# A two-layer graph kernel on one core: four pieces of a step's side work get other places in the order, one 8-bit tile a third buffer, and one addition another engine

## The chip, the core and the metric

The kernel runs on one core of one Trainium2 chip. A core has a matrix engine (TensorE; PE in the profile, its weight loads PEld), VectorE (DVE), ScalarE (ACT), GpSimd (POOL) and SyncE (SP), which issues most of the loads. Each engine takes its instructions strictly in its own order; between engines there are only semaphores. The metric is device time in microseconds (us): the median of the runs of one kernel. Lower is better.

## The reference, cut to what matters

There are N = 3327 rows x of width D = 512 and an adjacency matrix adj (0 or 1, about 1% ones). Twice a graph attention layer is applied, then a residual and a layer norm; a second, binary layer and another layer norm follow:

```python
def _gat_layer(x, W, adj):
    Wh, Ws = jnp.split(x @ W, 2, axis=-1)
    a = jax.nn.softmax(Wh @ Ws.T, axis=-1) * adj
    return jax.nn.leaky_relu(a @ Wh + x, 0.01)
h = _gat_layer(_gat_layer(x, W[0], adj), W[1], adj)
x = _layernorm(x + h)                      # "x +" is the input added to finished rows
bw, ba = sign(weight), maximum(sign(x), 0)
out = _layernorm(x + relu(adj @ (ba @ bw.T)))
```

The work is in `Wh @ Ws.T` (3327 x 3327 scores), the exponential of them, the mask, and `a @ Wh`.

## The kernel before, in words

**Tiling.** Rows are cut into 26 tiles of 128, and pairs of tiles make NQ = 13 groups g of 256 columns. A *step* is a pair (g, q): a 256 x 256 block of scores. The list `steps` has 169 of them, all q of g = 0 first. Each layer of attention (`attention(l, att)`, l = 0 and 1) runs over v, the index of the step whose values are multiplied (`values`, L1103 and on: seven products of a Strassen scheme, each 128x256, in `one`, L1120). Scores are made 31 half steps ahead (`LOOK`), so v starts below zero; those early steps have no values to multiply and are about half as long.

**Scores.** Of the 26 half steps of a chunk of two groups, 20 are made by `quad_scores` (five blocks of 4 half steps, 26 products each, L820), the other six by an ordinary Strassen scheme (L781). The products accumulate in banks of PSUM called P, Q, R, S, T, V (quad) or X, Y, Z; the pool `ps_ch` has only three. An intermediate result is taken from a bank, and more products then go into it, or another name gets the bank. It is taken out either by a ScalarE copy (`keep_as`, L826) or by a VectorE addition (`out`, L832; these are *a block's additions*). TensorE cannot add into the bank again until that is done. So a late L832 or L826 stops TensorE.

**The side work of a step**, for a block that was scored before:
- `shift`, L1044, VectorE: subtracts the column maximum (`beside`, which lies in PSUM) from the block, for step v+3.
- `exponential`, L1050, ScalarE, step v+3 (for q = 0 also L1049, the first term of the running total).
- `running`, L1055, VectorE: adds the block to the running total, step v+2.
- `masked`, L1060, VectorE: times adj, step v+2; behind it `sums`, L1093 to L1096, four GpSimd operations that make Strassen's left sides in a tile with three buffers.
- `narrow`, L1068, ScalarE: casts the adjacency block to 8 bits into the tile `adj_b` (two buffers); `degrees`, L1073, GpSimd; `exact`, L1083, VectorE; one step later `keep_blocks`, L1076, a GpSimd DMA that writes the 8-bit block to HBM. This happens in about every second step.
- `maximum`, L879, VectorE; `column_max` (L972 to L996), once for each group.
- When a group's last q is done, `take_out` (L1146 to L1157) reads its values from PSUM, and `finish` hands out one item a step: `scaled` (L1185), `leaky` (L1193), `stored` (in layer 1 the addition of the input, L1202, and then a GpSimd DMA, L151), `statistics` (L1215, L1216), `signs` (L1222, L1229).

**The order** is written by hand. Each step collects pairs of a place and a function, sorts them by place, and calls them; every engine's queue then is that order. Place 0 is the step's first product, 1 its last. Products have places too: value i has (i + 0.5)/7, the n-th product of a quad block (n + 0.5)/6.5 counted over its four half steps, and its addition comes 0.082 later. The lines that place the side work (L1379 to L1385):

```python
at = 0.12 if v >= 0 else 0.33 if v < -2 else 0.45
work += [(0.0, lambda: shift(*s3)), (at, lambda: exponential(*s3))]
...
work += [(0.2, lambda: running(*s2)), (0.48, lambda: masked(*s2))]
...
(0.6, lambda: narrow(*of)), (0.61, lambda: degrees(*of)), (0.66, lambda: exact(*of)),
...
if later and (last or v + 2 not in blocks or len(later) > 5 - v % NQ // 2):
    work += [(0.8, later.pop(0))]
```

`later` holds what `finish` handed out, `after` what goes to the next step (`keep_blocks` at 0.5). After both layers the binary layer's products (`aggregate`, L1471, and `linear`, L1564) end the kernel.

Of the kernel before, what the change touches and what calls it, by code (L numbers as in the profile page):

```python
# [11 lines left out]
F8 = mybir.dt.float8e4  # L12
# [3 lines left out]
ALU = mybir.AluOpType  # L16
# [3 lines left out]
P = 128  # L20
# [3 lines left out]
HW = CW // 2  # L24
# [21 lines left out]
def kernel(  # L46
# [8 lines left out]
    nc = tc.nc  # L55
# [6 lines left out]
    NQ = NT // 2  # L62
# [8 lines left out]
    def halves_of(c):  # L71
        return [g for g in (2 * c, 2 * c + 1) if g < NQ]

    def dense(c):
        return 0 < c and len(halves_of(c)) == 2 and c < NC

    def half_tiles(g):

        return (2 * g, 2 * g + 1)
# [16 lines left out]
    def slot(shape, dtype, name):  # L96
        return ring.tile(shape, dtype, tag="s", bufs=SBUFS, name=name)
# [609 lines left out]
    def attention(l, att):  # L707
# [173 lines left out]
        def scores(c, q, s):  # L881

            if dense(c) and q // 2 in quads:
                if (q % 2, s) == (0, 0):
                    quad_scores(c, q // 2)
                return []
            mine = halves_of(c)
            if s == 0:
                for i in mine:
                    sc[i, q] = slot([P, 2, HW], F32, f"s_{l}_{i}_{q}")  # L890
            w = len(mine) * P
            lo, hi = sc[mine[0], q][:, :, :w], sc[mine[-1], q][:, :, HW - w :]
            c11, c21, c12, c22 = lo[:, 0], lo[:, 1], hi[:, 0], hi[:, 1]

            def copied(name, bank):
                ch[name] = att.tile([P, w], F32, tag=name, bufs=1, name=f"{name}_{l}_{c}_{q}")
                nc.scalar.copy(ch[name], ch[bank])

            def z1():
                product(c, q, "Z", A11, B11, True)  # L900
                ch["X"] = ps_ch.tile([P, w], F32, tag="ch", name=f"pX_{l}_{c}_{q}")
                nc.scalar.copy(ch["X"], ch["Z"])

            def y5():
                product(c, q, "Y", S1, T1, True)
                copied("p5", "Y")

            def z6():
                product(c, q, "Z", S2, T2, False)
                copied("u2", "Z")  # L910

            def y3():
                product(c, q, "Y", S4, B22, False)

            def add12():
                nc.vector.tensor_tensor(c12, ch["Y"], ch["u2"], ALU.add)

            def z7():
                product(c, q, "Z", S3, T3, False)

            def add22():
                nc.vector.tensor_tensor(c22, ch["Z"], ch["p5"], ALU.add)  # L922

            def x2():
                product(c, q, "X", A12, B21, False)
                nc.scalar.copy(c11, ch["X"])

            def z4():
                product(c, q, "Z", A22, T4, False)
                nc.scalar.copy(c21, ch["Z"])  # L930

            if s == 1:

                after.append((-0.05, lambda: maximum(mine[0], q)))
                if q == NQ - 1:

                    plans = [
                        ((1, -0.04), (1, 0.2), (1, 0.6), (2, 0.16), (2, 0.17)) if mine[0] == 0
                        else ((1, -0.04), (1, 0.2), (1, 0.7), (2, 0.02), (2, 0.3)),
                        ((2, 0.68), (5, 0.83), (6, 0.83), (7, 0.83), (8, 0.83)),  # L940
                    ]
                    for i, plan in zip(mine, plans):
                        for (n, at), do in zip(plan, column_max(i)):
                            early.setdefault(v + n, []).append((at, do))
            if s == 0:
                return [(0.06, z1), (0.31, y5), (0.56, z6), (0.81, y3), (0.94, add12)]
            return [
                (0.02, z7), (0.15, add22), (0.35, x2), (0.68, z4),
            ] + [(0.62, lambda i=i: maximum(i, q)) for i in mine[1:]]
# [91 lines left out]
        def shift(g, q):  # L1041
            s = sc[g, q]
            at = beside[l][:, 0:1]
            nc.vector.tensor_tensor(s, s, at.to_broadcast([P, 2, HW]), ALU.subtract)  # L1044

        def exponential(g, q):
            if q == 0:
                total[g] = att.tile([P, 2, HW], F32, tag="total", name=f"total_{l}_{g}")
                nc.scalar.activation(total[g], sc[g, q], AF.Exp)  # L1049
            nc.scalar.activation(sc[g, q], sc[g, q], AF.Exp)  # L1050

        def running(g, q):

            if q > 0:
                nc.vector.tensor_tensor(total[g], total[g], sc[g, q], ALU.add)  # L1055

        def masked(g, q):

            s = sc[g, q]
            nc.vector.tensor_tensor(s, s, adj[g, q], ALU.mult)  # L1060
            sums(g, q, s)

        def narrow(g, q):

            t = adj[g, q, "b"] = att.tile(
                [P, 2, HW], F8, tag="adj_b", bufs=2, name=f"ab_{l}_{g}_{q}"
            )
            nc.scalar.copy(t, adj[g, q], saturate=False)  # L1068

# [89 lines left out]
        def finish(g):  # L1159
# [6 lines left out]
            mine = half_tiles(g)  # L1166
            held = {}
# [29 lines left out]
            def stored(i):  # L1197
                t, hh = mine[i], hs[i]
                r = rows(t)
                span = slice(t * P, t * P + r)  # L1200
                if last:
                    nc.vector.tensor_tensor(hh[:r], hh[:r], held[i, "x0"][:r], ALU.add)  # L1202
                load_rows(nc.gpsimd, h_d[span, :] if last else x1_d[span, :], hh, r)

            def residual(i):
# [56 lines left out]
        if last:  # L1262
# [14 lines left out]
            for n, e in enumerate(some):  # L1277
                at = n * (n1 - n0) / len(some)
# [59 lines left out]
        mine = [i for i, e in enumerate(steps) if e[1] % L == l]  # L1338
# [9 lines left out]
        for v in range(-LOOK - 4, len(steps)):  # L1348
            u = v + LOOK

            if 0 <= v + WS - 1 < len(steps):
                load_ws(*steps[v + WS - 1])
            if 0 <= v + 4 < len(steps):
                load_adj(*steps[v + 4])
            if v + 4 in blocks and (v + 4 < 0 or blocks[v + 4] != steps[v + 4]):
                load_adj(*blocks[v + 4])
            if 0 <= u + 2 < len(ahead):
                c, q, h = ahead[u + 2]
                if h == 0:
                    load_xs(c, q)  # L1360
            if u == -4:
                load_gs(0, 0, 7)

            c, i = divmod(u, 2 * NQ)
            if 0 <= c < NC - 1 and 22 <= i < 25:
                load_gs(c + 1, 2 * i - 44, 1 if i == 24 else 2)
            if dense(c) and i == 0 and quads:
                for n, at, do in query_sums(c):
                    early.setdefault(v + n, []).append((at, do))
            work, after = after, []  # L1370
            if 0 <= c < NC - 1 and i == 2 * NQ - 1:
                work += [
                    (at, lambda c=c, n=n: load_gs(c + 1, n)) for n, at in ((5, 0.43), (6, 0.8))
                ]
            if 0 <= v + 3 < len(steps):
                s3 = steps[v + 3]
                if not any(s3):
                    work.append((-0.02, lambda: spread(0)))
                at = 0.12 if v >= 0 else 0.33 if v < -2 else 0.45  # L1379
                work += [(0.0, lambda: shift(*s3)), (at, lambda: exponential(*s3))]  # L1380
                if s3[1] == NQ - 1 and s3[0] + 1 < NQ:
                    work.append((0.9, lambda: spread(s3[0] + 1)))
            if 0 <= v + 2 < len(steps):
                s2 = steps[v + 2]
                work += [(0.2, lambda: running(*s2)), (0.48, lambda: masked(*s2))]  # L1385
            if v + 2 in blocks:
                of = blocks[v + 2]
                work += [
                    (0.6, lambda: narrow(*of)), (0.61, lambda: degrees(*of)),
                    (0.66, lambda: exact(*of)),  # L1390
                ]
                after.append((0.5, lambda of=of: keep_blocks(*of)))
            if later and (last or v + 2 not in blocks or len(later) > 5 - v % NQ // 2):
                work += [(0.8, later.pop(0))]
            if 0 <= u < len(ahead):
                work += scores(*ahead[u])
            if v >= 0:
                work += values(*steps[v])
            work += early.get(v, [])
            for _, do in sorted(work, key=lambda e: e[0]):  # L1400
                do()
            if v >= 0 and steps[v][1] == NQ - 1:
                later += finish(steps[v][0])
            if last:
                load_products(v)
# [337 lines left out]
```

## Time and profile before

| | |
|---|---|
| median of 3 runs | 2499.78 us (2499.44 to 2500.13) |
| the profiled execution's own time | 2498.87 us |
| its span, first to last instruction | 2497.1 us |
| granted TensorE clock | 0.999 |
| TensorE busy | 2471.4 us (99%), 12052 matmuls |
| VectorE / ScalarE / GpSimd busy | 2031.8 (81%) / 852.9 (34%) / 1505.6 us (60%) |
| DMA | 635.89 MB |

A row of a group reads: line, engine, operation, written<-read tiles, shapes, count, then busy us and mean ns of one, then the idle time of the engine just before these instructions and what ended it. A row of the timeline reads: start, length, engine, line, operation, tiles, count, and in brackets the idle time before and what ended it. The trace shows each 128x256 matmul as 379 ns long, though the next one starts 216 ns after it: they overlap, so lost time of TensorE is read from the starts.

### The profile page before, as it was taken

The numbers are of one execution on the slowest core, as the hardware profiler recorded it, in microseconds if no ns is written. First come the engines' busy times: TensorE is split into PE (matmuls) and PEld (weight loads), VectorE is DVE, ScalarE is ACT, GpSimd is POOL, SyncE is SP. The second block draws the span as 40 slices with busy tenths as digits, with TensorE's granted clock in tenths as the row PEclk, the third lists the DMA queues.
The fourth block names the chain that finished last, engine by engine and source line by source line (L and its number), as shares of the span: only waits on it lengthen the run. The fifth ranks groups of instructions, "written<-read, shape, count | busy, mean of one in ns | idle before, by whom it ended". The sixth has DMA issues, their size and how long they took to land.

```text
span 2497.1 us, 39159 instructions
## 1 busy us (share of the span) xinstructions
PE 2471.4 (99%) x12052; PEld 2140.4 (86%) x12052; DVE 2031.8 (81%) x4005; ACT 852.9 (34%) x2127; POOL 1505.6 (60%) x2487
## 2 busy tenths in 40 slices
PE   9999999999999999999999999999999999999998
PEld 7888888888888888998888888888888888899886
DVE  6864788888988988768886588988889898888876
ACT  3333433333333333322233333333333333332234
POOL 3772566767677676545677256666666666655631
PEclk9999999999999999999999999999999999999999
DMA  6976767676677766897797676767767677688985
GB/s 209 322 267 222 249 236 253 233 262 236 239 253 236 266 230 231 294 317 258 244 334 270 225 260 220 269 223 265 241 232 270 227 268 240 230 283 301 317 279 174
DMA packets 318149, 635.89 MB, mean 255 GB/s; under 512 B 34317, under 2 KB 182405, under 8 KB 317934
## 3 DMA queue, kind: packets, MB, share of 16 engines
q1 hardware_dynamic: 289454, 540.93, 64.9%
q0 software_dynamic: 28480, 92.40, 9.6%
q8 instruction: 98, 1.61, 0.3%
q14 instruction: 117, 0.96, 0.1%
HBM read 521.98 MB, written 111.21 MB: 254 GB/s over the span
## 4 chain that ended last, share of the span: by engine, by line
PE 93%; DVE 4%; DMA 1%; issue 1%; ACT 1%; POOL 0%; SPq 0%; ACTq 0%; DVEq 0%; POOLq 0%
PE acc L1120 38%; PE pZ L781 9%; PE pP L820 6%; PE pQ L820 6%; PE pY L781 5%; PE pR L820 4%; PE pZ_wh L547 4%; PE pZ_g L612 3%; PE agg L1471 3%; PE pX L781 2%; PE pY_wh L547 2%; PE pY_g L612 2%; PE pT L820 2%; PE pS L820 1%; PE pm L439 1%; PE pV L820 1%
## 5 line engine op out<-in xcount | busy, mean ns | idle before, releaser
L1093 POOL TENSOR_TENSOR as<-s 128x128 f32<-128x128 f32 x338 | 210.9, 624 | 563.3 <-DVE s L1060 424.6
L1120 PE MATMUL acc<-ws,s 128*128 128x256 f32 x1352 | 402.3, 379 | 0.0
L1120 PE MATMUL acc<-ws,as 128*128 128x256 f32 x1352 | 380.5, 379 | 0.0
L1120 PE MATMUL acc<-wh,s 128*128 128x256 f32 x1352 | 380.0, 379 | 0.0
L1050 ACT ACTIVATE s<-s 128x512 f32<-128x512 f32 x338 | 213.2, 631 | 399.5 <-DVE s L1044 397.6
L1073 POOL TENSOR_TENSOR deg<-deg,adj 128x256 fp8e4<-128x256 fp8e4 x338 | 263.6, 780 | 44.5 <-DMA adj<-in_adjT_dram 29.7
L1120 PEld LDWEIGHTS acc<-ws,as 128*128 128x128 f32 x1352 | 251.4, 190 | 37.0 <-issue 3.1
L1120 PEld LDWEIGHTS acc<-wh,s 128*128 128x128 f32 x1352 | 252.5, 190 | 32.5
L1120 PEld LDWEIGHTS acc<-ws,s 128*128 128x128 f32 x1352 | 251.4, 190 | 33.1
L1055 DVE TENSOR_TENSOR total<-total,s 128x512 f32<-128x512 f32 x312 | 263.4, 844 | 0.0
L1060 DVE TENSOR_TENSOR s<-s,adj 128x512 f32<-128x512 f32 x338 | 242.5, 717 | 2.6 <-DMA adj<-in_adjT_dram 0.3
L879 DVE TENSOR_TENSOR top<-top,s 128x512 f32<-128x512 f32 x286 | 224.0, 786 | 23.4 <-ACT s L930 21.3
L781 PE MATMUL pZ<-ga,xs 128*128 128x256 f32 (+1 forms) x1096 | 234.3, 340 | 2.1 <-DVE s L922 1.7
L1044 DVE TENSOR_TENSOR s<-s,beside 128x512 f32<-128x512 f32 x338 | 227.7, 674 | 2.5 <-ACT beside L1039 2.5
L1094 POOL TENSOR_TENSOR s<-s 128x128 f32<-128x128 f32 x338 | 207.4, 614 | 26.7
L781 PEld LDWEIGHTS pZ<-ga,xs 128*128 128x128 f32 x1096 | 191.4, 190 | 26.4 <-DVE s L922 2.5
L1095 POOL TENSOR_TENSOR as<-s 128x128 f32<-128x128 f32 x338 | 191.3, 566 | 26.5
L1096 POOL TENSOR_TENSOR as<-s,as 128x128 f32<-128x128 f32 x338 | 185.3, 548 | 26.5
L1120 PE MATMUL acc<-wh,as 128*128 128x256 f32 x676 | 201.2, 379 | 0.0
L826 ACT COPY s<-pP 128x256 f32<-128x256 f32 x200 | 74.3, 372 | 249.6 <-PE pP L820 217.3
L1120 PEld LDWEIGHTS acc<-wh,as 128*128 128x128 f32 x676 | 125.7, 190 | 20.2 <-issue 3.6
L1076 POOL DMA_DIRECT2D adj_d<-ab x169 | 94.0, 556 | 78.5 <-ACT ab L1068 58.0
(274 smaller groups left out, 4969.6 us busy)
## 6 DMA issues: line engine op xcount, KB each, us to landing
ws<-ws_d SPq DMA_DIRECT2D x338, 512.0 KB
adj<-in_adjT_dram SPq DMA_DIRECT2D x351, 256.0 KB
xs<-xq_d SPq DMA_DIRECT2D x100, 832.0 KB
xs<-xs_d SPq DMA_DIRECT2D x82, 512.0 KB
xs<-xs_d SPq DMA_DIRECT2D x82, 384.0 KB
gs_d<-gsp POOLq DMA_DIRECT2D x84, 256.0 KB, 3.8
xq_d<-xq POOLq DMA_DIRECT2D x20, 832.0 KB, 4.7
ga<-gs_d SPq DMA_DIRECT2D x54, 256.0 KB
```

The costliest lines, as they stand in the source:

```text
L781: nc.tensor.matmul(ch[bank], xs[c, q, a][:, k], query(c, b)[:, k], start=(start and k == 0), stop=(k == 1), skip_group_check=True,)
L820: nc.tensor.matmul(bank[b], xs[c, i, f"x{r}"], right, start=r in begins, stop=True, skip_group_check=True,)
L879: nc.vector.tensor_tensor(top[i], top[i], t, ALU.max)
L1044: nc.vector.tensor_tensor(s, s, at.to_broadcast([P, 2, HW]), ALU.subtract)
L1050: nc.scalar.activation(sc[g, q], sc[g, q], AF.Exp)
L1055: nc.vector.tensor_tensor(total[g], total[g], sc[g, q], ALU.add)
L1060: nc.vector.tensor_tensor(s, s, adj[g, q], ALU.mult)
L1073: nc.gpsimd.tensor_tensor(deg[:, g], deg[:, g], adj[g, q][:, a], ALU.add, saturate=False)
L1093: nc.gpsimd.tensor_tensor(s3, a11, a21, ALU.subtract)
L1094: nc.gpsimd.tensor_tensor(a21, a21, a22, ALU.add)
L1095: nc.gpsimd.tensor_tensor(s2, a21, a11, ALU.subtract)
L1120: nc.tensor.matmul(acc[g][i // 2][:, i % 2], a[i], b[i], start=(q == 0 and i % 2 == 0), stop=(q == NQ - 1), skip_group_check=True,)
```

## The change

Within a step, `shift` moves from place 0.0 to 0.25, `exponential` from 0.12 (0.33 or 0.45 in the steps below zero) to 0.75, `running` from 0.2 to 0.475. The tile of the 8-bit adjacency block gets three buffers in place of two. In `column_max` of the first group, `across` moves from place 0.6 to 0.97 of its step. In layer 1, `stored` adds the input to the finished rows with GpSimd for the groups g < NQ - 3 = 10 (20 of the 26 additions), and with VectorE as before for the last three. Lines behind L1202 have numbers higher by one in the changed kernel.

```diff
-                        ((1, -0.04), (1, 0.2), (1, 0.6), (2, 0.16), (2, 0.17)) if mine[0] == 0
+                        ((1, -0.04), (1, 0.2), (1, 0.97), (2, 0.16), (2, 0.17)) if mine[0] == 0
...
             t = adj[g, q, "b"] = att.tile(
-                [P, 2, HW], F8, tag="adj_b", bufs=2, name=f"ab_{l}_{g}_{q}"
+                [P, 2, HW], F8, tag="adj_b", bufs=3, name=f"ab_{l}_{g}_{q}"
             )
...
                 if last:
-                    nc.vector.tensor_tensor(hh[:r], hh[:r], held[i, "x0"][:r], ALU.add)
+                    eng = nc.gpsimd if g < NQ - 3 else nc.vector
+                    eng.tensor_tensor(hh[:r], hh[:r], held[i, "x0"][:r], ALU.add)
                 load_rows(nc.gpsimd, h_d[span, :] if last else x1_d[span, :], hh, r)
...
-                at = 0.12 if v >= 0 else 0.33 if v < -2 else 0.45
-                work += [(0.0, lambda: shift(*s3)), (at, lambda: exponential(*s3))]
+                work += [(0.25, lambda: shift(*s3)), (0.75, lambda: exponential(*s3))]
...
-                work += [(0.2, lambda: running(*s2)), (0.48, lambda: masked(*s2))]
+                work += [(0.475, lambda: running(*s2)), (0.48, lambda: masked(*s2))]
```

## The prediction, as it was put on record

> **What bounds the kernel now.** I read the page's busy shares first, then what TensorE waited for, then the timeline around the longest waits. The page says that TensorE is the bound:
>
> ```profile
> PE 2471.4 (99%) x12052; PEld 2140.4 (86%) x12052; DVE 2031.8 (81%) x4005; ACT 852.9 (34%) x2127; POOL 1505.6 (60%) x2487
> ```
>
> So no other engine's time counts, except where it stops TensorE. To find these stops I took the distance from one matmul's start to the next and set it against the usual one of its shape (216 ns for 128x256 in float32). Distances beyond it sum to 28.6 us in the whole trace. That is the most any reordering could win. By place: loading and projecting 2.6 us, the start of layer 0's attention (268 to 285 us) 4.1, the rest of layer 0 1.3, the gap between 0.8, the start of layer 1's attention (1450 to 1467 us) 4.2, the rest of that (1540 to 2171 us) 14.1, the tail 1.5. After each real wait the next matmul is late by another 0.104 us; that is in these sums.
>
> What TensorE waited for (engine, line, waited for; total us, times, longest):
>
> ```profile
> PE pP L820 <- DVE s L832: 2.3, 6, 0.4
> PE pQ L820 <- ACT s L826: 2.2, 2, 1.5
> PE pP L820 <- ACT s L826: 2.0, 2, 1.3
> ...
> PE pR L820 <- DVE s L832: 1.5, 3, 0.8
> ```
>
> Everywhere it is a PSUM bank not yet emptied: by a block's addition on VectorE (L832) or a ScalarE copy (L826). The view counts only what exceeds a matmul's shown end, so it is smaller than my sum.
>
> Two places show what the addition and the copy stood behind. First VectorE and TensorE at 1856 us:
>
> ```profile
> 1855.54 0.67 DVE L1044 TENSOR_TENSOR s<-s,beside 128x512 f32<-128x512 f32 x1
> 1856.13 1.02 DVE L1055 TENSOR_TENSOR total<-total,s 128x512 f32<-128x512 f32 x1
> 1857.08 0.41 DVE L832 TENSOR_TENSOR s<-pQ,s 128x256 f32<-128x256 f32 x1
> 1857.41 0.41 DVE L832 TENSOR_TENSOR s<-pP,s 128x256 f32<-128x256 f32 x1
> ...
> 1857.88 0.70 PE L820 MATMUL pP<-gb,xs 128*128 128x256 f32 x2 [0.42 <-DVE s L832]
> ```
>
> The addition from bank P waits behind shift (L1044) and running total (L1055), neither of which anybody needs so soon. Second, ScalarE at 1668 us:
>
> ```profile
> 1668.43 0.62 ACT L1068 CAST ab<-adj 128x512 fp8e4<-128x512 f32 x1 [4.00 <-DMA adj_d<-ab]
> 1668.96 0.36 ACT L826 COPY s<-pQ 128x256 f32<-128x256 f32 x1
> ...
> 1669.38 0.70 PE L820 MATMUL pQ<-gb,xs 128*128 128x256 f32 x2 [1.52 <-ACT s L826]
> ```
>
> The cast to 8 bits waits 4.00 us for one of its two buffers to be written out, and the copy from bank Q waits behind the cast.
>
> **The change part by part**, for layer 1's 14.1 us, sorted by what ended each stop:
>
> *Third 8-bit buffer.* ScalarE waited 40.0 us in 17 places for these writes (longest 4.4); two of them reach TensorE, at 1669.38 and 2114.00: 1.68 + 0.84, and four times the tail of 0.104 or less, 2.73 us in all. The writes land in 1.8 to 6.8 us and blocks come about every second step (12 us), so with a third buffer none is waited for: -2.7 us. The copy then follows its product, and the addition behind it at 1669.41 moves up too.
>
> *Exponential at 0.75.* ScalarE waited 397.6 us in 197 places at L1050 for the shift, with copies queued behind it. Four such stops (pY behind L897; the longest 0.83 at 1593.31) make 1.48 us. With half a step (about 3 us) in place of 0.12 between shift and exponential they go: -1.5. Behind the exponential at its new place stand the copies at 0.85 and above; one is delayed by at most 0.63 us (the 631 ns of L1050's row), and its bank isn't wanted for another 1 us or more. Running total and mask want the exponential 0.72 of a step later.
>
> *Shift at 0.25, running at 0.475.* This puts a block's additions in the first half of a step ahead of 0.6 us of shift and 0.6 to 1.0 of running total (starts in the timeline follow each other by 0.60 for 128x512, 0.33 for 128x256). Stops of pV (2.51 us), pT (0.84), pR (1.02) and pY behind L832 (0.44) are each 0.24 us or less plus the tail, less than the work moved: -4.8. Four stops of pP (1620.98 and its like, 1.61 with tails) have shift alone ahead of the addition, and an excess under 0.4: -1.6. The five stops like the one shown (0.58 + 0.10 each, 3.4) lie where a group's values are taken out. Here running is also pushed behind L1147, which waits for ScalarE until 1850.41, so VectorE comes 0.6 later to this stretch; against it stand 1.0 us of running put behind the addition. I count half: -1.7.
>
> *The running total gets cheaper, too.* Its price depends on what GpSimd does: 680 ns where GpSimd stands still, 1021 ns where most of it lies beside L1073. Shift keeps 674 ns whatever GpSimd does; one of its operands is in PSUM.
>
> ```profile
> L1073 POOL TENSOR_TENSOR deg<-deg,adj 128x256 fp8e4<-128x256 fp8e4 x338 | 263.6, 780 | 44.5 <-DMA adj<-in_adjT_dram 29.7
> L1055 DVE TENSOR_TENSOR total<-total,s 128x512 f32<-128x512 f32 x312 | 263.4, 844 | 0.0
> L1060 DVE TENSOR_TENSOR s<-s,adj 128x512 f32<-128x512 f32 x338 | 242.5, 717 | 2.6 <-DMA adj<-in_adjT_dram 0.3
> L1044 DVE TENSOR_TENSOR s<-s,beside 128x512 f32<-128x512 f32 x338 | 227.7, 674 | 2.5 <-ACT beside L1039 2.5
> ```
>
> Next to the mask, where GpSimd mostly waits for the mask, I expect the running total near L1060's 717 ns, and some 40 us less of VectorE (312 x 0.127). It is no term of its own: it is what keeps the additions in time.
>
> *Addition of the input on GpSimd.* VectorE loses 20 x 0.876 us (L1202's mean). GpSimd gains 20 x at most 1.46 us, twice the 728 ns of L1162 for 128x256; below that nothing bounds it but VectorE's 0.685. Behind it in GpSimd's queue stand the rows' DMA and the next step's sums (L1093). GpSimd waited 424.6 us for L1060 at L1093, and TensorE wants the sums over a step later, so 1.46 us is hidden; the statistics come a whole step behind. Gain or loss for the sum: 0; if the cover were gone, 20 x 1.46 = 29 us at most.
>
> The Trainium skill speaks against this part. "GPSIMD Engine Reference", section 4.1, sends elementwise work on two tensors to VectorE, as GpSimd is about twice as slow; its 4497 ns for 2048 elements would make an estimated 1.1 us of 512, and by it the sum stays the same, since that too is hidden. "SBUF — State Buffer", section "Who interferes with whom", says that a VectorE instruction with two SBUF inputs contends with a GpSimd instruction that reads SBUF, and one with a single SBUF input does not; the 1021 against 680 ns and the steady 674 agree. By that rule the moved addition would slow a VectorE neighbour by up to its own length, taking back what VectorE was spared.
>
> *Layer 0 and the two starts.* Layer 0's pV and pR stops (1.2 us) go like those of layer 1: -1.1. At the starts, VectorE itself is late: between 275 and 281 us it works without a pause, and the order of that work stays, so the stop of 1.43 at 279.98 (a copy behind the exponential) goes but the next, at 281.39 for L832, grows by as much. Only layer 1's stop at 1466.74 (0.60) has shift and running ahead of its addition: -0.6. `across` at 0.97 lets one addition by (L916) and leaves L922, the one waited for at 268.18, where it was: 0.
>
> *New stops.* From 0.25 to 0.66 VectorE now has shift, running, mask and `exact` in one row (2.5 us) with additions between. Nothing in the trace has that; between 0 and 10 us, I take 2.
>
> Sum: 2.7 + 1.5 + 4.8 + 1.6 + 1.7 + 1.1 + 0.6 - 2 = 12.0 us less than the profiled execution's own 2498.87, which is 2486.9. The median of the runs is 0.9 above that execution, so I forecast **2487.8 us**.
>
> **The rivals.** *VectorE stays the bound of its stretches*: as at the starts, a stop that goes comes back at the next addition, since VectorE's total work in the crowded steps is what ends last. Then only ScalarE's two parts and layer 0 count: 2.7 + 1.5 + 1.1 = 5.3, less 1 to 2 of new stops, so some 2496. For it: from 1850.75 to 1868 VectorE never pauses. Against: it is then idle for 1.55 us before the next block, and is to lose work.
>
> *The crowd in the middle* (slower). Fillers that used to run while VectorE waited for early products now come later, and the additions of banks T and V late in a block miss their due place. Walking the last half step of a block: from 0.25 shift, addition, running, mask, addition take to 0.67, and T's bank is wanted at 0.92, so 0.25 of a step (1.5 us) is spare. If VectorE arrives over 1.5 us late, every block pays; at 0.4 us for each of the 50 blocks (the 50 of pV's additions) that is 20 us against 12 won: 2508. Against it: VectorE's lag behind its places is mostly under 1 us.
>
> *It does less than it says*: running total and mask wait for the later exponential, and nothing is gained or lost: about 2499.
>
> **How the numbers follow.** The forecast has 0.70, VectorE the bound 0.14, nothing 0.06, the crowd 0.10. The runs can tell 0.2% (5 us) from no change. Below 2494.8: the forecast and a third of the second case, 0.75; within: 0.15; slower: 0.10. The range: 2483 if nearly all of layer 1's 14 us go, no new stops come and part of a start; 2497 takes in the second case. The 10 us for new stops lie within it.
>
> **What would show it.** Right: no wait of L1068 for its DMA; L1050's 397.6 us cut by half or more; L1055 under 750 ns; TensorE's distances beyond the usual under 18 us, with pV and pT gone and the starts unchanged. Wrong: new waits of TensorE for L832 late in a step, VectorE idle at L1055 for ScalarE, or TensorE waiting for L1096.

## The result and the profile after

The changed kernel takes 2506.38 us (median of 19 runs, 2502.57 to 2507.95), the kernel before 2499.74 us (19 runs beside them, 2497.82 to 2501.62). The ratio is 1.0026, 95% interval 1.0020 to 1.0033: **slower by about 6.6 us**, where 12.0 us less was forecast. The time lies outside the predicted range and on the other side of no change. The profiled execution took 2504.88 us, its span is 2503.0 us (before: 2497.1). One run of e2 below took 6775.83 us and is left out of its median.

The page after says the same of the bound as before, with almost the same busy times:

```profile
PE 2478.3 (99%) x12052; PEld 2138.9 (85%) x12052; DVE 2036.7 (81%) x3985; ACT 842.8 (34%) x2127; POOL 1525.9 (61%) x2507
```

VectorE executes 20 instructions fewer and is busy 4.9 us longer. What TensorE waited for in the changed kernel (engine, line, waited for; total us, times, longest):

```profile
PE pS L820 <- DVE qu L832: 1.9, 3, 0.9
...
PE pT L820 <- DVE s L832: 1.1, 6, 0.2
```

The two waits for a ScalarE copy (pQ and pP behind L826), 4.2 us together, are gone. Bank S (the addition `qu<-pS`), which had no wait before, is now the second row of this view, and bank T has a row as well. The distances between matmul starts beyond the usual ones, the measure of the prediction, sum to 34.1 us after against 28.5 before: 5.6 more, and the spans differ by 5.9. So the loss is there, in us (all such sums are of one profiled execution each):

| | before | after |
|---|---|---|
| loading and projecting, gap, tail | 4.9 | 4.1 |
| start of layer 0 / of layer 1 | 4.1 / 4.2 | 5.6 / 3.7 |
| rest of layer 0 / of layer 1 | 1.3 / 14.1 | 5.8 / 14.9 |
| in the two rests: bank S | 0 | 8.1 |
| bank T | 0.8 | 6.0 |
| bank P | 5.1 | 5.0 |
| banks Q / V / Y | 2.7 / 3.4 / 1.9 | 0 / 0 / 0 |

What the change was to remove went (8.0 us at Q, V and Y), and 13.3 us of something new came, at S and T. At the start of layer 0 some 1.7 of the 5.6 us are no wait: just behind a stop of bank R (1.96 us, at 281.38) the granted clock fell to half for 3.41 us, and the matmuls' starts lie 427 ns apart instead of 216. In the view by stretches (start and end, length, busy us and count of each engine, clock, DMA's share and GB/s):

```profile
282.42:285.83 3.41, 3.41 (x10) 2.70 (x9) 3.38 (x6) 1.12 (x3) 2.58 (x6) 0.50 0.96 334
```

The profile before has no such stretch between its first and its last microseconds. The groups of the changed kernel:

```profile
L1060 DVE TENSOR_TENSOR s<-s,adj 128x512 f32<-128x512 f32 x338 | 259.0, 766 | 10.8
L1073 POOL TENSOR_TENSOR deg<-deg,adj 128x256 fp8e4<-128x256 fp8e4 x338 | 248.3, 735 | 44.8 <-DMA adj<-in_adjT_dram 30.1
L1055 DVE TENSOR_TENSOR total<-total,s 128x512 f32<-128x512 f32 x312 | 243.6, 781 | 0.1
L1044 DVE TENSOR_TENSOR s<-s,beside 128x512 f32<-128x512 f32 x338 | 227.7, 674 | 1.1 <-ACT beside L1039 1.1
```

The running total (L1055) fell from 844 to 781 ns only, and the mask (L1060) rose from 717 to 766; the shift (L1044) keeps its 674. Rows not shown say that ScalarE's part went as told: the cast (L1068) no longer waits for its DMA (40.0 us before), and the exponential (L1050) waits 224.7 us for the shift in place of 397.6.

Now the changed kernel's timeline around one stop of bank S (start, length, engine, line; in brackets the idle time before and what ended it):

```profile
1883.11 0.42 DVE L832 TENSOR_TENSOR s<-pQ,s 128x256 f32<-128x256 f32 x1 [1.14 <-PE pQ L820]
...
1884.04 0.42 DVE L832 TENSOR_TENSOR s<-pP,s 128x256 f32<-128x256 f32 x1 [0.51 <-ACT pQ L829]
...
1884.38 0.94 DVE L1055 TENSOR_TENSOR total<-total,s 128x512 f32<-128x512 f32 x1
...
1885.36 0.69 DVE L1060 TENSOR_TENSOR s<-s,adj 128x512 f32<-128x512 f32 x1
...
1885.97 0.69 DVE L879 TENSOR_TENSOR top<-top,s 128x512 f32<-128x512 f32 x1
...
1886.57 0.42 DVE L832 TENSOR_TENSOR qu<-pS,qu 128x256 f32<-128x256 f32 x1
...
1887.04 0.70 PE L820 MATMUL pS<-ga,xs 128*128 128x256 f32 x2
```

and the same block in the kernel before, VectorE's rows alone:

```profile
1878.53 0.94 DVE L1055 TENSOR_TENSOR total<-total,s 128x512 f32<-128x512 f32 x1
1879.56 0.42 DVE L832 TENSOR_TENSOR s<-pQ,s 128x256 f32<-128x256 f32 x1
1880.49 0.42 DVE L832 TENSOR_TENSOR s<-pP,s 128x256 f32<-128x256 f32 x1 [0.51 <-ACT pQ L829]
1880.83 0.68 DVE L1060 TENSOR_TENSOR s<-s,adj 128x512 f32<-128x512 f32 x1
1881.43 0.68 DVE L879 TENSOR_TENSOR top<-top,s 128x512 f32<-128x512 f32 x1
1882.03 0.42 DVE L832 TENSOR_TENSOR qu<-pS,qu 128x256 f32<-128x256 f32 x1
```

Read from the addition of P to that of S: 1.54 us before, 2.53 after. The 0.99 between the two is the running total, behind whose start the next instruction starts 0.98 later. In both kernels VectorE cannot begin this row sooner, because P's addition stands behind a wait of 0.51 us for L829. Before, the running total was done by then, ahead of Q's addition. After, VectorE stands idle for 1.14 us ahead of Q's addition with the running total still in its queue behind. S's next product waits for the late addition: 0.25 us, and 0.10 more for the start after a wait.

The stop of bank T in the next half step has the same origin. The second addition from P and the one from T, after and then before:

```profile
1887.51 0.42 DVE L832 TENSOR_TENSOR s<-pP,s 128x256 f32<-128x256 f32 x1
...
1892.26 0.42 DVE L832 TENSOR_TENSOR s<-pT,s 128x256 f32<-128x256 f32 x1
...
1892.73 0.70 PE L820 MATMUL pT<-gb,xs 128*128 128x256 f32 x2 [0.17 <-DVE s L832]
```
```profile
1882.97 0.42 DVE L832 TENSOR_TENSOR s<-pP,s 128x256 f32<-128x256 f32 x1
...
1887.56 0.41 DVE L832 TENSOR_TENSOR s<-pT,s 128x256 f32<-128x256 f32 x1
```

Between the two VectorE does the same work in another order and does not wait, in either kernel (4.59 us before, 4.75 after). So the 0.99 us by which it came late out of the half step before reaches T's addition, and T's product pays 0.33 us (by the starts) and 0.10.

That VectorE idles early and is late afterwards is seen over the whole run in the group of the additions from Q, first before, then after (last column: idle time just before them, and what ended it):

```profile
L832 DVE TENSOR_TENSOR s<-pQ,s 128x256 f32<-128x256 f32 x150 | 61.7, 412 | 24.0 <-PE pQ L820 23.7
```
```profile
L832 DVE TENSOR_TENSOR s<-pQ,s 128x256 f32<-128x256 f32 x150 | 61.9, 413 | 40.0 <-PE pQ L820 39.9
```

The group of the additions from P goes from 22.1 us of idle time to 42.4 in the same way: 46 us ahead of these two groups became 82.

### The profile page after: what moved, and what is told of

It reads as the page before. It is cut to its first block, busy times and chain, and to the rows that moved or that the text cites. A ratio compares the mean times of both kernels' runs of the same rounds, so it can differ in the third digit from the quotient of the medians.

```text
span 2503.0 us, 39147 instructions
## 1 busy us (share of the span) xinstructions
PE 2478.3 (99%) x12052; PEld 2138.9 (85%) x12052; DVE 2036.7 (81%) x3985; ACT 842.8 (34%) x2127; POOL 1525.9 (61%) x2507
## 4 chain that ended last, share of the span: by engine, by line
PE 92%; DVE 6%; issue 1%; ACT 0%; DMA 0%; SPq 0%; ACTq 0%; DVEq 0%
PE acc L1120 38%; PE pZ L781 9%; PE pQ L820 6%; PE pP L820 6%; PE pY L781 5%; PE pR L820 4%; PE pZ_wh L547 4%; PE pZ_g L612 3%; PE agg L1471 3%; PE pX L781 2%; PE pY_wh L547 2%; PE pT L820 2%; PE pY_g L612 2%; PE pS L820 1%; PE pm L439 1%; DVE s L832 1%
## 5 line engine op out<-in xcount | busy, mean ns | idle before, releaser
L1050 ACT ACTIVATE s<-s 128x512 f32<-128x512 f32 x338 | 213.3, 631 | 225.9 <-DVE s L1044 224.7
L1073 POOL TENSOR_TENSOR deg<-deg,adj 128x256 fp8e4<-128x256 fp8e4 x338 | 248.3, 735 | 44.8 <-DMA adj<-in_adjT_dram 30.1
L1060 DVE TENSOR_TENSOR s<-s,adj 128x512 f32<-128x512 f32 x338 | 259.0, 766 | 10.8
L1055 DVE TENSOR_TENSOR total<-total,s 128x512 f32<-128x512 f32 x312 | 243.6, 781 | 0.1
L879 DVE TENSOR_TENSOR top<-top,s 128x512 f32<-128x512 f32 x286 | 221.8, 778 | 17.3 <-ACT s L930 15.5
L1044 DVE TENSOR_TENSOR s<-s,beside 128x512 f32<-128x512 f32 x338 | 227.7, 674 | 1.1 <-ACT beside L1039 1.1
L826 ACT COPY s<-pP 128x256 f32<-128x256 f32 x200 | 74.3, 372 | 225.6 <-PE pP L820 209.6
```

Source lines behind the costliest of these rows:

```text
L879: nc.vector.tensor_tensor(top[i], top[i], t, ALU.max)
L1073: nc.gpsimd.tensor_tensor(deg[:, g], deg[:, g], adj[g, q][:, a], ALU.add, saturate=False)
```

## The experiments

The theory from here on: the running total's new place is the cause; the other parts gain, but less than it loses. Rivals: the exponential's place holds VectorE up, the crowd has no single author, or GpSimd's addition is what lies in the way. All edits are against the kernel before (e1 to e4, e8) or the changed kernel (the others); times are medians, and each ratio is against the kernel before, run beside it.

### One part alone: e1 to e4

e1, the running total:

```diff
-                work += [(0.2, lambda: running(*s2)), (0.48, lambda: masked(*s2))]
+                work += [(0.475, lambda: running(*s2)), (0.48, lambda: masked(*s2))]
```

> Only the running total's place changes, 0.2 to 0.475. Crowd theory (the running total now stands with mask and maximum between the block's addition from bank P and the one from bank S, and TensorE waits for S): slower than before by 3 to 8 us, with about 50 stops of pS. Lock theory (GpSimd's long addition holds VectorE up): within 2 us of before, hardly a stop of pS. Shift theory (shift no longer fills VectorE's early waits): within 2 us of before or faster by up to 5.

Measured: 2518.40 us, ratio 1.0078 (1.0064 to 1.0092): 19 us slower, three times the loss of the whole change and far more than the 3 to 8 us expected. Not S alone pays: against before, the stops of T grew by 7.8 us, of S by 5.4, of P by 4.5 and of Y by 3.4, while V's 3.4 went. Its profile has the same row in a place where none of its instructions is stretched by GpSimd:

```profile
1661.34 0.42 DVE L832 TENSOR_TENSOR s<-pQ,s 128x256 f32<-128x256 f32 x1 [1.58 <-PE pQ L820]
...
1662.27 0.42 DVE L832 TENSOR_TENSOR s<-pP,s 128x256 f32<-128x256 f32 x1 [0.51 <-ACT pQ L829]
...
1662.61 0.68 DVE L1055 TENSOR_TENSOR total<-total,s 128x512 f32<-128x512 f32 x1
...
1664.54 0.42 DVE L832 TENSOR_TENSOR qu<-pS,qu 128x256 f32<-128x256 f32 x1
...
1665.02 0.47 PE L820 MATMUL pS<-ga,xs 128*128 128x256 f32 x1
```

From P's addition to S's it is 2.27 us, with mask and maximum again in between: a running total of the plain 0.68 us is enough for a late addition from S. The exponential has no share in it, being early in this kernel.

e2, shift and exponential:

```diff
-                at = 0.12 if v >= 0 else 0.33 if v < -2 else 0.45
-                work += [(0.0, lambda: shift(*s3)), (at, lambda: exponential(*s3))]
+                work += [(0.25, lambda: shift(*s3)), (0.75, lambda: exponential(*s3))]
```

> Only shift (0.25) and exponential (0.75) change place. Crowd theory: faster than before by 2 to 6 us, stops of pV and of pY behind the exponential gone, few of pS. Lock theory: the same. Shift theory: slower by 2 to 6 us, stops of pS or pT in most blocks.

Measured: 2499.01 us, ratio 0.9998 (0.9988 to 1.0007), no change. In its profile the stops of Y went (1.9 to 0) and those of V shrank (3.4 to 1.0), but bank Q waited 4.3 us for ScalarE, where the cast waits for its second buffer, against 2.7 before; behind the longer of these two stops, at 2111.08, the clock was half for 3.41 us, which cost another 1.7. The runs lie far apart: the two least, 2493.23 and 2493.74 us, have a mean granted clock of 0.998, the five from 2499.70 to 2502.11 us one of 0.996. Alone, then, this part gains nothing by the median; with the running total moved as well it is worth some 8 us (e8, below).

e3, the input's addition on GpSimd, and e4, the third buffer:

```diff
-                    nc.vector.tensor_tensor(hh[:r], hh[:r], held[i, "x0"][:r], ALU.add)
+                    eng = nc.gpsimd if g < NQ - 3 else nc.vector
+                    eng.tensor_tensor(hh[:r], hh[:r], held[i, "x0"][:r], ALU.add)
```
```diff
-                [P, 2, HW], F8, tag="adj_b", bufs=2, name=f"ab_{l}_{g}_{q}"
+                [P, 2, HW], F8, tag="adj_b", bufs=3, name=f"ab_{l}_{g}_{q}"
```

> Only the addition of the input to 20 of the finished tiles goes to GpSimd. Crowd and shift theory: within 2 us of before. Lock theory: slower by 3 to 6 us, with stops of TensorE beside most of the 20 additions.

> Only the third 8-bit buffer. All theories: the waits of the cast for its DMA (40.0 us in 17 places) go, and with them the stops of pQ at 1669 and 2114 us: 2 to 3 us faster than before. If the stops come back at the next addition: within 1 us.

Measured: e3 2500.84 us, ratio 1.0002 (0.9993 to 1.0011), no change; e4 2497.32 us, ratio 0.9990 (0.9981 to 0.9999), 2.0 us faster by the medians and 2.5 by the ratio (its interval goes from 0.2 to 4.7) beside 2.7 forecast for it, and the stops of bank Q for ScalarE are gone.

### The change without one part: e5 and e6

e5, the running total back at 0.2; e6, the input's addition back on VectorE:

```diff
-                work += [(0.475, lambda: running(*s2)), (0.48, lambda: masked(*s2))]
+                work += [(0.2, lambda: running(*s2)), (0.48, lambda: masked(*s2))]
```
```diff
-                    eng = nc.gpsimd if g < NQ - 3 else nc.vector
-                    eng.tensor_tensor(hh[:r], hh[:r], held[i, "x0"][:r], ALU.add)
+                    nc.vector.tensor_tensor(hh[:r], hh[:r], held[i, "x0"][:r], ALU.add)
```

> The changed kernel with the running total back at 0.2. Crowd theory: 5 to 12 us faster than before (third buffer 2, shift and exponential without the casts' waits 3 to 6, one addition less on VectorE), TensorE's distances beyond the usual 18 to 24 us, no stops of pS. Rival (the running total's place only uncovers that VectorE is too slow with GpSimd's addition beside it): no better than before.

> The changed kernel with the addition of the input back on VectorE. Crowd theory: as slow as the changed kernel within 3 us (2503 to 2509), pS stopped in about as many blocks, the long stops beside GpSimd's addition (0.9 and 1.1 us at 2044 and 2201 us) gone. Lock theory: back to before or faster (2495 to 2500).

Measured: e5 **2492.48 us**, ratio 0.9970 (0.9958 to 0.9982): 7 us faster than the kernel before. e6 2503.41 us, ratio 1.0018 (1.0009 to 1.0028), some 2 to 3 us below the changed kernel, and its interval overlaps the changed kernel's. So four of the five parts (shift and exponential counted as one) gain 7 us together, and the fifth turns that into a loss of 6.6. The same block in e5:

```profile
1876.49 0.94 DVE L1055 TENSOR_TENSOR total<-total,s 128x512 f32<-128x512 f32 x1
...
1878.92 0.42 DVE L832 TENSOR_TENSOR s<-pQ,s 128x256 f32<-128x256 f32 x1 [0.90 <-PE pQ L820]
1879.86 0.42 DVE L832 TENSOR_TENSOR s<-pP,s 128x256 f32<-128x256 f32 x1 [0.51 <-ACT pQ L829]
...
1881.40 0.42 DVE L832 TENSOR_TENSOR qu<-pS,qu 128x256 f32<-128x256 f32 x1
```

From P's addition to S's it is 1.54 us again, and no product of S waits in this block, although the shift stands at its new place. Bank S's stops fall from 8.1 to 0.4 us, bank T's from 6.0 to 0.3.

### Where to put it instead: e7 and e8

e7 moves running total and mask behind S's addition at 0.62; e8 leaves only the moves of running total, shift and exponential (buffer, `across` and the input's addition as before):

```diff
-                work += [(0.475, lambda: running(*s2)), (0.48, lambda: masked(*s2))]
+                work += [(0.625, lambda: running(*s2)), (0.63, lambda: masked(*s2))]
```

> The changed kernel with the running total at 0.625 and the mask at 0.63, behind the additions from banks S (0.62 in its step) and T (0.543). Crowd theory, if it is what stands ahead of these two additions that counts: no stops of pS and pT, 6 to 12 us faster than the changed kernel. If it is VectorE's idle time at the early additions that counts: as slow as the changed kernel or slower, the stops only move to other banks (pV, pR, pP).

> Before with the running total, shift and exponential moved, nothing else. Running total alone cost 19 us, the whole change 6.6. If shift at 0.25 gives the difference back (it fills VectorE's later time, so less stands ahead of pV, pT and pY): 2504 to 2509. If buffer and GpSimd do: 2514 to 2520.

Measured: e7 2509.47 us, ratio 1.0040 (1.0027 to 1.0054); e8 2510.51 us, ratio 1.0048 (1.0034 to 1.0062). In e7 the stops of S are gone and those of T down to 0.3 us, but bank P takes over: by the starts, its stops are 20.1 us in all. This is the second of the two outcomes named. An addition from P, at 2.774 of the block's four half steps, now has the row ahead of it (running total, mask and `exact`):

```profile
1817.53 0.41 DVE L832 TENSOR_TENSOR qu<-pS,qu 128x256 f32<-128x256 f32 x1
1817.87 0.79 DVE L1055 TENSOR_TENSOR total<-total,s 128x512 f32<-128x512 f32 x1
1818.69 0.69 DVE L1060 TENSOR_TENSOR s<-s,adj 128x512 f32<-128x512 f32 x1
...
1819.91 0.42 DVE L832 TENSOR_TENSOR s<-pP,s 128x256 f32<-128x256 f32 x1
...
1820.39 0.48 PE L820 MATMUL pP<-gb,xs 128*128 128x256 f32 x1 [0.37 <-DVE s L832]
```

A later place does not make room; it changes the bank that pays. e8 came out between the two ranges expected for it, nearer the first. Against e1: once the running total is late, the later shift and exponential give 8 us of 19 back; buffer, `across` and the input's addition make the rest of the way to 2506.38.

### The running total's place, step by step: e11, e12 and f1

The edit is the first number of the line above, in the changed kernel: 0.3 (e11), 0.0 (e12), 0.4 (f1).

> The kernel of e5 with the running total at 0.3: behind the additions from the banks S and P early in the step (0.08 and 0.236), still ahead of the waits for the products of Q and P at 0.313 and 0.467. Theory (what counts is whether the running total stands ahead of those two waits and so runs in time in which VectorE would idle, or behind them in a row with the mask): 2490 to 2494, ratio 0.996 to 0.998, no stops of bank S. Rival (every move to a later place costs in proportion to its length): a third or more of the 14 us between e5 and the changed kernel, 2497 to 2500, ratio 0.999 to 1.000.

> The kernel of e5 with the running total at the step's start, 0.0. Theory: still ahead of the waits at 0.313 and 0.467, so no stops of bank S in the second half, but the additions from S and P early in the step now stand behind 0.8 us more of work: stops of pV (0.69 us in e5) and of pY come back by 1 to 4 us, 2493.5 to 2497, ratio 0.9975 to 0.999. Rival (earlier is always better): as e5 or faster, ratio 0.997 or below.

> The changed kernel with the running total at 0.4: behind VectorE's wait for Q's product (0.313), ahead of that for P's (0.467), the addition from P between it and the mask. If standing behind the wait for Q is what costs: VectorE idles about 40 us ahead of the additions from Q, as in the changed kernel, stops of bank S remain, 2502 to 2506, ratio 1.001 to 1.0025. If only the row with the mask costs: about 2494, ratio 0.9975. If each of the two waits is a part of it: between, 2497 to 2501, since VectorE waits 0.51 us for P as well, time that the running total would then fill.

All else as in the changed kernel, so that e5 and the changed kernel belong to the row. The places of VectorE's additions in between are Q 0.313, P 0.467, S 0.62 in the third of a block's four half steps and P 0.236, Q 0.39, T 0.543 in the last. The kernel of e5 was profiled in the slowest of its six runs (2495.34 us):

| running total at | us | ratio to before (95%) | stops of S / T / P, us | idle ahead of Q's / P's additions, us |
|---|---|---|---|---|
| 0.0 (e12) | 2500.53 | 0.9998 (0.9989 to 1.0007) | 0.9 / 3.8 / 9.1 | 27.8 / 23.4 |
| 0.2 (e5) | 2492.48 | 0.9970 (0.9958 to 0.9982) | 0.4 / 0.3 / 4.7 | 26.1 / 33.0 |
| 0.3 (e11) | 2493.85 | 0.9974 (0.9962 to 0.9985) | 1.3 / 0.4 / 3.9 | 15.0 / 47.5 |
| 0.4 (f1) | 2498.48 | 0.9996 (0.9987 to 1.0005) | 1.9 / 1.3 / 7.7 | 41.2 / 31.2 |
| 0.475 (changed) | 2506.38 | 1.0026 (1.0020 to 1.0033) | 8.1 / 6.0 / 5.0 | 40.0 / 42.4 |

Moving from 0.2 to 0.3 costs about 1 us, less than the intervals, though the running total passes P's addition at 0.236 and the shift. Behind the wait for Q (0.4) it costs 6, behind the wait for P and next to the mask (0.475) 14. f1 parts these last two, and each is a share: the outcome "between". At f1 my view had to be narrowed. VectorE's idle time ahead of Q is as long there as in the changed kernel (41.2 and 40.0 us), yet 8 us of the loss are gone. So idle time before Q is the sign, not the cost. The same block in f1 shows why:

```profile
1878.97 0.42 DVE L832 TENSOR_TENSOR s<-pQ,s 128x256 f32<-128x256 f32 x1 [1.13 <-PE pQ L820]
1879.31 0.68 DVE L1055 TENSOR_TENSOR total<-total,s 128x512 f32<-128x512 f32 x1
1879.91 0.42 DVE L832 TENSOR_TENSOR s<-pP,s 128x256 f32<-128x256 f32 x1
```

P's addition starts 0.94 us after Q's here as well (0.93 in both kernels shown above): the running total, 0.60 from start to start, just fills the 0.51 that VectorE otherwise waits for L829. At 0.475 it stands behind that wait and is paid in full.

e12 shows that earlier is not always better either; its 2500.53 us lies above both outcomes expected. At 0.0 the addition from S at the step's head stands behind the running total, and one beside GpSimd's L1073 takes 1.60 us (e12; T's next product waits for this bank and starts 1.06 us late, at 1971.97):

```profile
1969.98 1.60 DVE L1055 TENSOR_TENSOR total<-total,s 128x512 f32<-128x512 f32 x1
1971.50 0.41 DVE L832 TENSOR_TENSOR s<-pS,s 128x256 f32<-128x256 f32 x1
```

### The starts, GpSimd, and the best parts: e9, e10 and f2

e9 is e5 with shift and exponential at their old places ahead of a layer's first block; e10 is e5 with the input's addition on VectorE; f2 is both. The line of e9 and f2:

```diff
-                work += [(0.25, lambda: shift(*s3)), (0.75, lambda: exponential(*s3))]
+                to, at = (0.25, 0.75) if v >= 0 else (0.0, 0.33 if v < -2 else 0.45)
+                work += [(to, lambda: shift(*s3)), (at, lambda: exponential(*s3))]
```

> All of the change but the running total's new place (as in the kernel of e5), and in the steps ahead of a layer's first block (v below 0) the shift and the exponential back at their old places. Theory (only where in-order VectorE work stands counts): the stops at the two starts go from 5.6 and 5.2 us back to about 4.1 and 4.2, so 1 to 3 us less than e5's 2492.5: 2489.5 to 2491.5, ratio 0.996 to 0.9967. Rival (the starts are bound by the sum of VectorE's work, whatever its order): as e5, 2492 to 2493, ratio 0.997.

> The kernel of e5 with the input's addition back on VectorE. Theory A (GpSimd's 1.28 us addition holds VectorE's instructions with two SBUF inputs, and that costs more than the additions taken off VectorE): 2 to 3 us faster than e5, about 2490, ratio 0.996. Theory B (off the path on both engines): as e5, ratio 0.9965 to 0.9975. Theory C (VectorE needs the relief): 1 to 3 us slower than e5, ratio 0.9975 to 0.998.

> The running total at its old place 0.2, shift and exponential at their old places in the steps ahead of a layer's first block, the input's addition on VectorE; what is left of the change is the third buffer, the later shift and exponential, and the later place in column_max. If the gains of e9 and e10 add up: 2488 to 2491, ratio 0.9955 to 0.996. If the input's addition on GpSimd is worth nothing either way: as e9, ratio 0.996.

Measured: e9 2490.39 us, ratio 0.9959 (0.9945 to 0.9972); e10 2491.72 us, 0.9963 (0.9949 to 0.9976); f2 2489.57 us, 0.9957 (0.9944 to 0.9971). In e9 the starts fall to 3.8 and 3.5 us, from 5.8 and 5.2 in e5; of these 3.7 us, 0.7 is a DMA in e5 and some 3.4 are two stretches of half clock, one at each start of e5, which e9 has not. The times agree, but the intervals of e5 and e9 overlap. e10's interval holds e5's time, and f2's holds e9's: which engine adds the input cannot be told from the time once the running total stands well. The least medians, f2's and e9's, are about 10 us below the kernel before and 16 to 17 below the changed one. The distances beyond the usual ones are 20.0 us in e9, 21.7 in f2.

## Why the prediction was wrong, point by point

**The failed step is "New stops."** It said "From 0.25 to 0.66 VectorE now has shift, running, mask and `exact` in one row (2.5 us) with additions between. Nothing in the trace has that; between 0 and 10 us, I take 2." Measured: 13.3 us more at S and T than before (14.1 in all), over the upper bound. The walk behind it, written down in the rival "The crowd in the middle", went from 0.25 on with VectorE always busy, found T's addition done at 0.67 and 1.5 us spare. Two things are missing there. In the half step before the last, VectorE is not free to work through: P's addition at 0.467 waits for TensorE and for L829, so the row of running total, mask and maximum (L879, left out of the walk) starts from there, however idle VectorE was before. And in that row bank S is late, while only T and V were walked. In the last half step of the block shown VectorE does work without a pause, as the walk took it, but it enters it 0.99 us late, and T's addition is late by that. Both could have been read in the trace of before: the idle time of 0.51 at P's addition, and the running total in the idle time ahead of Q's.

**The rival that named the crowd** had the side, the kind (additions from a bank late in a block behind fillers) and nearly the time (2508 against 2506.38), but a chance of 0.10 and the wrong condition. VectorE need not arrive over 1.5 us late: in the block shown it arrives 1.14 us early.

**"The running total gets cheaper, too"** failed as well. It was to take 717 ns next to the mask and takes 781; mask and `exact` (L1083: 782 to 825) rose instead. VectorE was to be some 40 us less busy, and some 17 more for the input's additions; it is 4.9 us more. Added up by their own lengths, VectorE's instructions are 21 us less (2273 to 2252), 18 of it the input's additions: what the running total saved (20) the mask (17) and `exact` (7) took back. The busy time counts rows that overlap once, and they overlap less in the changed kernel (215 us in place of 241).

**The other terms**, with the running total left in place (e5), were to give 14.0 us by my sum and gave 7.0:
- Third buffer: -2.7 forecast, -2.0 to -2.5 measured alone (e4). Right.
- Exponential: its four stops of Y are gone (1.48 us). Right within the change. Shift and exponential without the buffer gain nothing by the median, and in e2's profile the cast then stops bank Q for longer.
- Stops of V, T, R and Y behind L832, -4.8: right in sign. In e5 some 1.9 us are left in layer 1, at V, T, R, S and Q.
- The pP stops, -3.3: from 5.1 to 3.2 us in layer 1 of e5, so -1.8.
- Layer 0, -1.1: from 1.3 to 1.7 us. V's stops there went and P's came (1.4 us).
- The starts, -0.6: from 8.3 to 11.0 us in e5 (0.7 of it a DMA). "The order of that work stays" was wrong: in the early steps, which are half as long, shift at 0.25 instead of 0.0 is behind other work of VectorE, and one addition from R keeps TensorE waiting for 2.12 and 2.22 us in one piece. What the sum had no term for is the clock: behind each of these two stops it fell to half for 3.41 us, which cost some 3.4 us in all. Without that e5's starts, at about 6.9 us without the DMA, would be shorter than before. The old places there (e9) bring the starts to 7.3 us, with no half clock.
- `across` 0: the stop at L922 shortened from 1.00 to 0.87 us. Right.
- Input on GpSimd, 0: not told from 0 alone (e3) and in e10; in the crowded order of the changed kernel it may cost 2 to 3 us (e6), but the intervals overlap.

So the two terms that ScalarE made (4.2 us) were sized well. The four that needed VectorE to be early (4.8, 3.3, 1.1 and 0.6, together 9.8) gave 2.9 + 1.8 - 0.4 - 2.7 = 1.6 by this count; the starts alone account for 3.3 of the difference, which is what the half clock cost. The count is of e5's slowest run: its span is 3.6 us below the one before, where the medians differ by 7.0.

**What would have shown it**: of the signs given for "right", no wait of L1068 for its DMA, and V gone, came true; L1050's wait was cut by 43%, less than the half; L1055 stayed over 750 ns, the starts changed, T grew, and the distances are 34.1 us and not under 18. The first sign given for "wrong", new waits for L832 late in a step, is what the trace shows.

Not tried: running total and mask apart, with the mask behind T's addition. Why the running total costs 6 us at 0.4, where it fills the wait in the block shown, was read only in part: P's two longest stops in f1 are 0.98 us each, at 1701.83 and 1857.29 us (in e5 the second is 0.50, at 1857.24).

## What to carry to other kernels

An engine that takes its instructions in order needs filler work *ahead* of the instruction at which it will wait; moved behind it, the filler adds its whole length to what follows, up to the next wait, though the busy share does not change. Before moving an instruction, look up in the timeline where its engine idles and which instruction ends that wait, and walk from that instruction, not from the place written in the code, to every bank's deadline. Several moves made at once can hide one bad one: taking one part out at a time found 7 us of gain under a loss of 6.6.

## What the runs showed of the hardware

GpSimd's addition of 128x512 in float32 takes 1272 ns at least (median 1278, longest 1722, 20 of them), under the bound of 1.46 us. A VectorE instruction with two inputs in SBUF that meets it is held for almost its whole length, here `exact`, some 0.68 us when alone:

```profile
1916.43 1.89 DVE L1083 SCALAR_TENSOR_TENSOR dull<-adj 128x512 fp8e4<-128x512 f32 x1
1916.48 1.28 POOL L1203 TENSOR_TENSOR h<-h,x 128x512 f32<-128x512 f32 x1
```

This happened four times to L1083 (1.89 to 1.90 us) and three times to L1060 (1.64 to 1.65); once it held the maximum (L879, 1.76). Five times GpSimd's is stretched itself, to 1.72 us, when a running total or a mask has begun up to 0.43 us ahead of it. Shift and additions, which have one operand in PSUM, keep their 0.68 and 0.42 us beside it. The Trainium skill, "SBUF — State Buffer", section "Who interferes with whom", says that a VectorE instruction with two SBUF inputs contends with a GpSimd instruction that reads SBUF, and calls the shared pair of ports "an exclusive lock". These rows agree: 0.68 and 1.28 us of work that meet take about 1.9 us here. So a VectorE instruction that stands ahead of a bank's addition can be late by a microsecond through GpSimd alone: the two longest stops of bank S in the changed kernel (0.93 us at 2044.08, 1.11 us at 2201.13) stand behind masks of 1.64 and 1.65 us.

**A long stop of TensorE is often followed by half the clock.** From the start of layer 0's attention to the end of layer 1's, the 16 profiles have 19 single stops of TensorE of 2.1 to 3.0 us, measured by the starts. Behind 11 of them the granted clock is 0.50 for 3.41 us, and in each such stretch the matmuls lose another 1.3 to 1.8 us. Behind none of the shorter stops (up to 1.71 us) is there such a stretch. Of the 19, 18 are bank R's at the two starts, all in kernels that move the shift there; what decides between the 11 and the other 8 these runs do not show. So one long stop can cost more than the same time in two short ones: before, the start of layer 0 has stops of 1.43 and 0.45 us, and the clock stays.
